# Expert pairs planned up to 12 slots behind the last scan, with GpSimdE storing the last ones, and earlier loads in the final stage

## The chip, the cores and the metric

The kernel runs on one core of one Trainium2 chip. The metric is device time in microseconds (us); lower is better. Everything is float32.

The engines are named here as in the profile: PE is TensorE (matmuls), PEld its weight loads, DVE is VectorE, ACT is ScalarE, POOL is GpSimdE, SP is SyncE, which here only issues transfers (DMAs). POOL also issues some. Each engine executes its instructions in program order.

## The reference, cut to what matters

Two batches of 256 channels by 64 x 64 positions (4096 tokens) go through a scan layer, then a layer of two scans (forward and flipped), then a mixture of 8 experts with soft weights:

```python
x = x + _L0_conv_ref(_gn(x), ...)            # selective scan, 256 inner channels
t = _to_tokens(x)
t = t + _L1_attn_ref(_ln_t(t), ...)          # two selective scans, 512 inner channels, one flipped
t = t + _L1_ffn_ref(_ln_t(t), ...)           # mixture of experts

def _L1_ffn_ref(x, ...):
    feat = jnp.mean(x, axis=0)               # mean over the two batches
    w = jax.nn.softmax(feat @ Wr + br, axis=-1)
    h = relu(bn(einsum('bfd,edh->bfeh', x, W1) + b1))
    h = relu(bn(einsum('bfeh,ehk->bfek', h, W2) + b2))
    y = jnp.einsum('bfeh,ehd->bfed', h, Wo) + bo
    return jnp.einsum('bfed,fe->bfd', y, w)  # weighted sum over the 8 experts
```

The point that shapes the kernel: an expert's three products depend on one batch's tokens alone, but the weight `w` of an expert for a token needs the mean over both batches, so it is known only when both batches have left the scans.

## The kernel before, in words

**Tiles.** Each batch's 4096 tokens are 8 chunks of 512 (`T`); a tile holds 128 partitions by 2 channel halves (`KC`) by 512. A *pair* is one expert applied to one chunk of one batch: 2 batches x 8 chunks x 8 experts = 128 pairs. Each pair has three products (layers 0, 1, 2 with W1, W2, Wo); each has two output halves `m`, and one half of one layer, an *entry* below, is four MATMUL instructions of the trace (two halves of the inner dimension, each float32 product showing as two MATMULs), so 24 per pair.

**First stage, the scans.** Six scan jobs (three per batch) are cut into chunks and *quads*; the main loop over `g` runs 640 quads with two *slots* each, 1280 slots in all. In each slot DVE does one scan instruction (L690), ACT the two exponentials it needs (L664), POOL or DVE the products before and behind it (L654, L699, L715), PE the sum over states (L723). All other work is put into slots by hand: `Slots.put(slot, queue, fn)` files a function under a slot and a queue, and in each slot the loop runs the queues `sp`, `pe`, the sums, `pe2`, the decays on ACT, `act`, the scan, `dve`, and `pool` in this order. The order is kept on each engine (`in_order`). A slot number is thus an order of issue and not a time: SP runs ahead of the others where no buffer holds it up.

**Features.** When a chunk of a flipped job is finished, `features` (L781 to L820) normalises it for the experts: a mean on PE, `fcen` on DVE, squares `fsq` on ACT (L799), a variance `fvar` on PE (L804), the root on ACT, the division on DVE, and a store to `nf_dram`. Offsets in slots are written out in one tuple. The very last flipped chunk (batch 1, chunk 0) has no such step.

**Experts beside the scans.** `experts` (L847) is a planner: it walks the slots up to `last` and keeps running balances of PE's and ACT's work (`PE_ROOM`, `PE_BEHIND`, `ACT_ROOM`, `ACT_BEHIND`) and of PSUM banks (`fits`). It places the six entries of each pair in order, and follows rules on distance: `waits` says that a layer's first entry comes at least 5 slots behind the same layer's last entry of the pair before (6 for layer 0 at a new chunk), because each layer's weights have one buffer (`ew0`, `ew1`, `ew2`), loaded 3 slots behind their last use. Complete pairs are kept (`put`) and given out by `emit_experts` (L905): weights by SP (L932), products on `pe2` (L912), relu or copy on ACT (L923, L921), and the unweighted result `eu`, one buffer, stored by SP into `u_dram` (L942) 3 slots behind the last entry. `early[b, c]` counts the pairs of a chunk that are done this way.

Behind the main loop come the last sum, the last gate and `sl.run_all(2 * nq, 2 * nq + 10)`, which runs what is filed in slots from 1280 on: before, the last chunk's output products (L759, L761 in slots 1283 and 1284), their copies (L776) and the store to `t_dram` (L777).

**Last stage, the rest of the experts.** The first stage's SBUF and PSUM pools close and new ones open. Chunks whose 16 pairs are all done form `whole`; the others form `rest`. For `rest` the remaining pairs run one after another on PE: `layer` (L1196) for layers 0 and 1 (L1201, relu L1205 on ACT), `weigh` (L1211) multiplies with the expert's weight on DVE (L1212), and `last_layer` (L1214) adds Wo's product into PSUM (L1220); a chunk's last pair adds PSUM to `x` (L1225) and stores. `waiting` holds the pairs between their layers and their last layer: a pair is weighed one pair later and goes through its last layer two pairs later.

Between the pairs the lists `side[i]` give out pieces of other work: `routes` (load features `n` by POOL L1086, sum over batches `nm` on POOL L1108, logits L1115, softmax, transposed weights, their store and broadcast load `wb` of 2 MB on POOL's queue L1144, L1146) for the chunks to come, and `sums` (load `x` L1156, bias L1163 to L1166, and for each pair done early `add_early` L1168: load `u` by SP L1170, times weight L1171 and added to `x` L1172 on DVE, then the store L1175). `u` has 3 buffers.

With the plan of before, 74 pairs are done beside the scans: `whole` is chunk 7, and chunk 6 has its batch 0 and two experts of batch 1. The last stage runs 54 pairs: 6 of chunk 6, then 8 (batch 1) of each of the chunks 5 to 0.

Of the kernel before, what the change touches and what calls it, by code (L numbers as in the profile page):

```python
# [42 lines left out]
F32 = mybir.dt.float32  # L43
# [4 lines left out]
P = 128  # L48
# [83 lines left out]
def hybrid_kernel(ctx: ExitStack, tc: tile.TileContext, a: dict, out: bass.AP):  # L132
# [53 lines left out]
    with ExitStack() as st:  # L186
# [594 lines left out]
        def features(b, c, v, s0):  # L781

            featured.add((b, c))

            def mean():
                v["ps"] = psp.tile([P, T], F32, tag="ps", name=f"fmean_{b}{c}")
                for k in range(KC):
                    nc.tensor.matmul(
                        v["ps"], mean_w, v["x"][:, k, :], start=(k == 0), stop=(k == KC - 1)
                    )  # L790

            def centre():
                v["cen"] = wk.tile([P, KC, T], F32, tag="cen", name=f"fcen_{b}{c}")
                nc.vector.tensor_tensor(v["cen"], v["x"], over_channels(v["ps"]), ALU.subtract)

            def square():
                for k in range(KC):
                    v["sq", k] = wk.tile([P, T], F32, tag="th", name=f"fsq_{b}{c}{k}", bufs=3)
                    nc.scalar.activation(v["sq", k], v["cen"][:, k, :], AF.Square)  # L799

            def variance():
                v["var"] = psp.tile([P, T], F32, tag="ps", name=f"fvar_{b}{c}")
                for k in range(KC):
                    nc.tensor.matmul(  # L804
                        v["var"], mean_w, v["sq", k], start=(k == 0), stop=(k == KC - 1)
                    )

            def divide():
                nc.vector.tensor_tensor(v["cen"], v["cen"], over_channels(v["var"]), ALU.mult)

            for d, queue, fn in (
                (0, "pe", mean), (1, "dve", centre), (2, "act", square), (3, "pe", variance),
                (4, "act", lambda: rsqrt(v["var"], v["var"], eps5)), (5, "dve", divide),
                (6, "sp", lambda: nc.sync.dma_start(nf_dram[b][:, c, :, :], v["cen"])),
            ):
                sl.put(s0 + d, queue, fn)
            sl.count(s0, 2, 0, (1,))
            sl.count(s0 + 1, 0, 2)
            sl.count(s0 + 3, 2, 2, (2,))
            ready.append((s0 + 8, b, c))  # L820

        def scales():

# [22 lines left out]

        def experts():  # L847

            last = 2 * nq - 6
            banks = sorted(sl.banks, key=lambda r: r[0])  # L850

            def fits(slot):
# [16 lines left out]
            def follows(l):  # L869

                k, m = divmod(len(times[l]), KC)
                if k == len(todo):
                    return None
                waits = [(l - 1, k * KC + 1, 2)] if l else []
                if m:
                    waits.append((l, k * KC, 0))
                elif k:

                    waits.append((l, k * KC - 1, 6 if l == 0 and todo[k][-1] == 0 else 5))
                    if l < 2:  # L880
# [24 lines left out]
        def emit_experts(put):  # L905
# [31 lines left out]
                n[b, c] = wk.tile([P, KC, T], F32, tag="en", name=f"en_{b}{c}")  # L937
                nc.sync.dma_start(n[b, c], nf_dram[b][:, c, :, :])

            def store(b, c, e, key):  # L940
                u = u_dram[b, c, e] = drp.tile([P, KC, T], F32, name=f"u_{b}{c}{e}")
                nc.sync.dma_start(u, key["u"])  # L942

            for b, c, e, times in put:
                key = {"tag": f"{b}{c}_{e}"}
# [5 lines left out]
                for l, (x, dst) in enumerate((("n", "h1"), ("h1", "h2"), ("h2", "u"))):  # L951
                    at = before.get(l, times[0] - 6) + 3
                    sl.put(at, "sp", lambda l=l, e=e, key=key: load_w(l, e, key["tag"]))
                    for m in range(KC):
# [1 line left out]
                        pe, act = layer(x, dst, l, m, e, key)  # L956
                        sl.put(slot, "pe2", pe)
                        sl.put(slot + 1, "act", act)
                sl.put(times[-1] + 3, "sp", lambda b=b, c=c, e=e, key=key: store(b, c, e, key))


        ready = []
# [92 lines left out]
            in_order()  # L1055
        emit_sum(g)
        emit_gate(i, steps[i][0].nj - 1)
        sl.run_all(2 * nq, 2 * nq + 10)
        assert not sl.at


    with ExitStack() as st:
# [12 lines left out]
        for i in range(NCH - 1, -1, -1):  # L1075
            (whole if all(first[b, i] == E for b in range(NB)) else rest).append(i)

        def load_n(i):

            for b in range(NB):  # L1080
                n[b, i] = mk.tile([P, KC, T], F32, tag="n", name=f"n_{i}{b}", bufs=6)
                if (b, i) in featured:
                    src = nf_dram[b][:, i, :, :]
                else:
                    src = t_dram[b][:, :, i * T : (i + 1) * T]
                nc.gpsimd.dma_start(n[b, i], src)  # L1086
# [107 lines left out]
            nc.sync.dma_start(we[name, e], a[name][e].rearrange("(k p) n -> p k n", p=P))  # L1194

        def layer(x, l, e, tag):  # L1196
            h = mk.tile([P, KC, T], F32, tag=f"h{l}", name=f"h{l}_{tag}", bufs=2 + l)
            for m in range(KC):
                ps = psp.tile([P, T], F32, tag="ps", name=f"hp{l}_{tag}_{m}")
                for k in range(KC):  # L1200
# [10 lines left out]
        def weigh(b, i, e, h):  # L1211
            nc.vector.tensor_tensor(h, h, over_channels(wb[i][:, e, :]), ALU.mult)  # L1212
# [39 lines left out]
        nc.sync.dma_start(bo, a["bo"])  # L1252
        layer_norm(rest[0])
        both(rest[0])
        weights = [("Wo", order[0])]
        for k in range(2, E):
            weights += [("W1", order[k]), ("W2", order[k]), ("Wo", order[k - 1])]
# [5 lines left out]
        for at, (b, i, e) in enumerate(pairs):  # L1263
# [6 lines left out]
                logits(i)  # L1270
            elif at == 1:
                spread(i)
            if waiting:
                weigh(*waiting[-1])
            waiting.append((b, i, e, h))
            if len(waiting) > 2:
                last_layer(*waiting.pop(0))
            done[i] += 1
            work = side[i] if at > 1 else []
# [111 lines left out]
```

## Time and profile before

| what | value |
|---|---|
| median of 3 runs | 5184.88 us (5181.89 to 5185.45) |
| the profiled execution | 5183.55 us |
| its span, first to last instruction | 5181.8 us |
| mean granted PE clock | 0.917 |
| first scan, last scan (start) | 61.1 us, 4498.2 us |
| mean time of one slot between them | 3.47 us |
| first matmul of the last stage | 4527.3 us |
| last matmul instructions end | 5176.4 us |

In section 2 of the page the span is cut into 40 slices of 130 us; in the first 34 of them DVE and POOL stand mostly at 9 tenths, and in the last 5 PE alone does. So the kernel has two stages with different limits, and a row of the whole page mixes them; it has to be read by window.

A row of the windows table gives for each engine its busy time and, in brackets, its number of instructions, then the granted PE clock, the busy share of the 16 DMA engines, and GB/s. A line of the chain gives the start, the length, and the piece of work that the end of the program hung on at that moment. A line of the waits gives the waiting engine and line, whom it waited for, the total in us, how often, and the longest.

### The profile page before, as it was taken

What the parts mean: (1) busy time and instruction counts of PE and PEld (TensorE: products, weight loads), DVE (VectorE), ACT (ScalarE), POOL (GpSimd) and SP (SyncE); (2) the same over time, 40 slices, a digit from 0 to 9 for tenths busy, and PEclk for the clock granted to TensorE, in tenths of its full rate; (3) what the DMA queues carried; (4) which work ended last, traced back from release to release, by engine and by line L of the source; (5) the groups of instructions that cost most, each with busy time, mean ns of one, the idle gap of its engine ahead of it and who ended that gap; (6) DMA issues with size and microseconds to landing.
All of it is one profiled execution on the core that took longest, in us unless ns stands there. A gap on an engine that the chain in (4) does not pass through costs nothing. (4 is left out here: it accounts for less than half of the span.)

```text
span 5181.8 us, 47299 instructions
## 1 busy us (share of the span) xinstructions
PE 4292.9 (83%) x14920; PEld 1483.9 (29%) x14920; DVE 4577.8 (88%) x3083; ACT 3681.3 (71%) x7462; POOL 4410.4 (85%) x1438
## 2 busy tenths in 40 slices
PE   5677677766668898888888888889899899689999
PEld 1222122222122233332222233223333333234444
DVE  6998999999999999999989999999999999746333
ACT  5778677777767888888887788888788888522332
POOL 5998999999999999999989999999999999611010
PEclk8888888887889999999999999999999999889999
DMA  4454433344334554555555544455544555354322
GB/s 176 154 178 163 154 127 139 129 152 154 135 131 160 195 185 164 182 171 196 191 185 177 191 159 174 155 181 191 178 165 165 173 183 175 117 189 155 111 104 77
DMA packets 314731, 834.47 MB, mean 161 GB/s; under 512 B 35240, under 2 KB 102064, under 8 KB 272496
## 3 DMA queue, kind: packets, MB, share of 16 engines
q1 hardware_dynamic: 310768, 806.15, 45.1%
q0 software_dynamic: 3712, 25.30, 1.3%
q8 instruction: 118, 1.93, 0.1%
q14 instruction: 133, 1.09, 0.1%
HBM read 647.18 MB, written 184.16 MB: 160 GB/s over the span
## 5 line engine op out<-in xcount | busy, mean ns | idle before, releaser
L654 POOL TENSOR_TENSOR bq<-rxdt,bc 128x2048 f32<-128x2048 f32 x640 | 2893.3, 4543 | 26.9 <-issue 11.8
L664 ACT ACTIVATE da<-rdt,w_a 128x512 f32<-128x512 f32 x2560 | 1756.5, 686 | 98.4 <-DVE bq L690 53.0
L690 DVE TENSOR_TENSOR_SCAN da<-da,h_state,bq 128x1024 f32<-128x1024 f32 x664 | 1559.2, 2348 | 63.8 <-ACT da L664 34.4
L715 POOL TENSOR_TENSOR bq<-bq,bc 128x2048 f32<-128x2048 f32 (+1 forms) x280 | 1180.0, 4214 | 22.5
L690 DVE TENSOR_TENSOR_SCAN bq<-da,h_state,bq 128x1024 f32<-128x1024 f32 x456 | 1058.6, 2338 | 20.3 <-ACT da L664 20.2
L723 PE MATMUL y<-bq,stack 128*32 128x512 f32 x5120 | 765.4, 691 | 347.4 <-POOL bq L715 324.1
L699 DVE TENSOR_TENSOR bq<-da,bc 128x1024 f32<-128x1024 f32 x760 | 926.5, 1219 | 15.9
L912 PE MATMUL e<-eh,ew 128*128 128x512 f32 x1184 | 578.6, 619 | 59.1 <-ACT eh L923 16.9
L709 ACT COPY h_state<-da 128x2 f32<-128x2 f32 x759 | 119.5, 157 | 680.0 <-DVE bq L699 678.5
L675 ACT ACTIVATE bq<-h_state,bq,a 128x1 f32<-128x1 f32 x1120 | 430.0, 384 | 0.7 <-POOL bq L654 0.2
L1205 ACT ACTIVATE h<-hp,of,sc 128x512 f32<-128x512 f32 x216 | 167.9, 778 | 347.4 <-PE hp L1201 330.3
L723 PEld LDWEIGHTS y<-bq,stack 128*32 128x32 f32 x5120 | 144.0, 118 | 906.1 <-POOL bq L715 461.1
L452 PE MATMUL conv<-xs,w_conv 64*64 64x512 f32 x2560 | 329.8, 604 | 24.4 <-ACT xs L436 21.4
L414 PE MATMUL z<-nx,w_in 128*128 128x512 f32 x640 | 324.7, 640 | 25.0 <-DVE sp L513 12.4
L414 PE MATMUL xs<-nx,w_in 128*128 128x512 f32 x640 | 317.5, 626 | 28.2 <-DVE xc L466 13.3
L912 PEld LDWEIGHTS e<-eh,ew 128*128 128x128 f32 x1184 | 214.2, 193 | 419.0 <-issue 209.0
L912 PE MATMUL e<-en,ew 128*128 128x512 f32 x592 | 286.1, 616 | 43.1 <-DVE sz L543 15.9
L761 PE MATMUL o<-sz,w_out 128*128 128x512 f32 x640 | 304.6, 616 | 0.0
L730 PE MATMUL y<-xc,w_d 128*128 128x512 f32 x320 | 193.6, 689 | 66.0 <-DVE sz L742 55.4
L517 POOL TENSOR_TENSOR xdt<-sp,xc 128x512 f32<-128x512 f32 x160 | 203.5, 1275 | 51.8 <-DVE sp L513 51.8
L923 ACT ACTIVATE eh<-e,of,sc 128x512 f32<-128x512 f32 x296 | 224.3, 770 | 30.5 <-PE e L912 29.9
L501 PE MATMUL dt<-dbc,w_dt 64*128 64x512 f32 x320 | 192.2, 695 | 41.2 <-ACT dbc L488 27.0
(138 smaller groups left out, 5045.5 us busy)
## 6 DMA issues: line engine op xcount, KB each, us to landing
rxdt<-xdtd SPq DMA_DIRECT2D x160, 1024.0 KB, 6.5
rdt<-dtd SPq DMA_DIRECT2D x160, 1024.0 KB, 6.3
bc<-bcd SPq DMA_DIRECT2D x384, 256.0 KB, 3.2
dtd<-sp SPq DMA_DIRECT2D x160, 256.0 KB, 3.6
xdtd<-xdt SPq DMA_DIRECT2D x160, 256.0 KB, 3.4
ew<-in_W SPq DMA_DIRECT2D x148, 256.0 KB, 4.9
u<-eu SPq DMA_DIRECT2D x74, 512.0 KB, 4.0
u<-u SPq DMA_DIRECT2D x74, 512.0 KB, 4.0
```

The costliest lines, as they stand in the source:

```text
L414: nc.tensor.matmul(ps, job.w["in", half][:, k, j * P : (j + 1) * P], rhs, start=(k == 0), stop=(k == KC - 1),)
L452: nc.tensor.matmul(v[r][64 * col : 64 * col + 64, :], job.w["conv"][rows, 2 * jp + j, k, :], ck["xs", jp][rows, j, k : k + T] if k < 4 els ...
L654: nc.gpsimd.tensor_tensor(bq[g], ck["rxdt", j], over_groups(ck["bc", 0, sg]), ALU.mult)
L664: nc.scalar.activation(da[g, h][:, k, :], cks[i]["rdt", j][:, q, :], AF.Exp, scale=steps[i][0].w["a"][:, j, q * SG + sg : q * SG + sg + 1],)
L675: nc.scalar.activation(bq[g][:, q, 0:1], job.h[:, j, sg, q : q + 1], AF.Identity, scale=cks[i]["a0", j][:, h, sg : sg + 1], bias=bq[g][:, ...
L690: nc.vector.tensor_tensor_scan(b if on_pool(g, h) else d, d, b, job.h[:, j, sg, 2 * h : 2 * h + 1] if c else 0.0, ALU.mult, ALU.add,)
L699: nc.vector.tensor_tensor(bq[g][:, two, :], d, cks[i]["bc", 1, sg].rearrange("p (o t) -> p o t", o=1).to_broadcast([P, 2, T]), ALU.mult,)
L715: nc.gpsimd.tensor_tensor(b, b, cks[i]["bc", 1, sg].rearrange("p (o t) -> p o t", o=1).to_broadcast([P, groups, T]), ALU.mult,)
L723: nc.tensor.matmul(y[i, j][q * CG : (q + 1) * CG, :], stack, bq[g][:, q, :], start=False, stop=(sg == SG - 1),)
L761: nc.tensor.matmul(v[m], job.w["out"][:, j, m * P : (m + 1) * P], ck["sz", j], start=False, stop=(j == job.nj - 1),)
L912: nc.tensor.matmul(ps, ew[l][:, k, m * P : (m + 1) * P], key[x][:, k, :], start=(k == 0), stop=(k == KC - 1),)
L923: nc.scalar.activation(key[dst][:, m, :], key["ps", l, m], AF.Relu, bias=of[:, l, e, m : m + 1], scale=sc[:, l, e, m : m + 1],)
```

## The change

1. In `features` the variance and all behind it move one slot later, and the chunk counts as ready at slot +9, not +8.
2. `experts` plans up to slot `2 * nq + 15`, not `2 * nq - 6`, so behind the last scan too, and lets a layer's first entry follow the same layer's last entry by 4 slots, not 5. `run_all` behind the loop runs up to `2 * nq + 24`.
3. A result `u` whose store falls behind slot `2 * nq - 8` is stored by GpSimdE's queue, not by SyncE's.
4. In the last stage `rest` is sorted by the number of pairs done; the features of the first whole chunk and of the second chunk of `rest` are loaded before the first pair; `h1` has 4 buffers, not 3; a pair waits three pairs, not two, for its last layer, and the first pairs are weighed later.

```diff
-                (0, "pe", mean), (1, "dve", centre), (2, "act", square), (3, "pe", variance),
-                (4, "act", lambda: rsqrt(v["var"], v["var"], eps5)), (5, "dve", divide),
-                (6, "sp", lambda: nc.sync.dma_start(nf_dram[b][:, c, :, :], v["cen"])),
+                (0, "pe", mean), (1, "dve", centre), (2, "act", square), (4, "pe", variance),
+                (5, "act", lambda: rsqrt(v["var"], v["var"], eps5)), (6, "dve", divide),
+                (7, "sp", lambda: nc.sync.dma_start(nf_dram[b][:, c, :, :], v["cen"])),
...
-            sl.count(s0 + 3, 2, 2, (2,))
-            ready.append((s0 + 8, b, c))
+            sl.count(s0 + 4, 2, 2, (2,))
+            ready.append((s0 + 9, b, c))
...
-            last = 2 * nq - 6
+            last = 2 * nq + 15
...
-                    waits.append((l, k * KC - 1, 6 if l == 0 and todo[k][-1] == 0 else 5))
+                    waits.append((l, k * KC - 1, 6 if l == 0 and todo[k][-1] == 0 else 4))
...
-                nc.sync.dma_start(u, key["u"])
+                by.dma_start(u, key["u"])
...
+                by = nc.gpsimd if times[-1] + 3 > 2 * nq - 8 else nc.sync
+                queue = "pool" if times[-1] + 3 > 2 * nq - 8 else "sp"
...
-        sl.run_all(2 * nq, 2 * nq + 10)
+        sl.run_all(2 * nq, 2 * nq + 24)
...
+        rest.sort(key=lambda i: sum(first[b, i] for b in range(NB)))
...
+            if (0, i) in n:
+                return
...
-            h = mk.tile([P, KC, T], F32, tag=f"h{l}", name=f"h{l}_{tag}", bufs=2 + l)
+            h = mk.tile([P, KC, T], F32, tag=f"h{l}", name=f"h{l}_{tag}", bufs=2 + 2 * l)
...
         both(rest[0])
+        for i in whole[:1] + rest[1:2]:
+            load_n(i)
...
-            if waiting:
-                weigh(*waiting[-1])
+            for p in {0: [], 1: [], 2: waiting[:1], 3: waiting[1:]}.get(at, waiting[-1:]):
+                weigh(*p)
             waiting.append((b, i, e, h))
-            if len(waiting) > 2:
+            if len(waiting) > 3:
                 last_layer(*waiting.pop(0))
```

More of the change, by code (lines that the diff above doesn't have):

```diff
@@ L938, in load_n, with store @@
                 nc.sync.dma_start(n[b, c], nf_dram[b][:, c, :, :])
-            def store(b, c, e, key):
+            def store(b, c, e, key, by):
                 u = u_dram[b, c, e] = drp.tile([P, KC, T], F32, name=f"u_{b}{c}{e}")
-                nc.sync.dma_start(u, key["u"])
+                by.dma_start(u, key["u"])
             for b, c, e, times in put:
@@ L958, in emit_experts @@
                         sl.put(slot + 1, "act", act)
-                sl.put(times[-1] + 3, "sp", lambda b=b, c=c, e=e, key=key: store(b, c, e, key))
+                by = nc.gpsimd if times[-1] + 3 > 2 * nq - 8 else nc.sync
+                queue = "pool" if times[-1] + 3 > 2 * nq - 8 else "sp"
+                sl.put(times[-1] + 3, queue, lambda b=b, c=c, e=e, key=key, by=by: store(b, c, e, key, by))
         ready = []
```

## The prediction

> **What bounds the kernel now.** I read the page first, for who is busy.
>
> ```profile
> PE 4292.9 (83%) x14920; PEld 1483.9 (29%) x14920; DVE 4577.8 (88%) x3083; ACT 3681.3 (71%) x7462; POOL 4410.4 (85%) x1438
> ...
> ew<-in_W SPq DMA_DIRECT2D x148, 256.0 KB, 4.9
> ```
>
> No engine stands out, because two stages are mixed. So next the windows of the last part:
>
> ```profile
> 4250.00:4502.00 252.00, 206.21 (x698) 70.93 (x700) 242.82 (x151) 192.88 (x398) 234.32 (x76) 0.92 0.44 153
> 4502.00:4527.00 25.00, 11.55 (x24) 4.20 (x24) 0.69 (x1) 1.17 (x2) 1.25 (x2) 0.70 0.36 121
> 4527.00:4700.00 173.00, 150.41 (x351) 65.80 (x352) 88.44 (x83) 43.91 (x61) 29.36 (x22) 0.89 0.57 201
> 4700.00:5182.00 482.00, 473.50 (x1146) 204.05 (x1145) 190.67 (x177) 144.48 (x193) 48.28 (x33) 1.00 0.30 104
> ```
>
> The columns are PE, PEld, DVE, ACT and POOL. Up to 4502 DVE is busy 96% and POOL 93%, PE 82%: the scans set the pace and PE has room. From 4527 PE alone is the bound (98% from 4700 on, DVE 40%). Between lie 25 us of crossing. A pair is nearly free in the first stage and costs its whole PE time in the last. The chain of waits shows the crossing:
>
> ```profile
> 4514.20 3.09 DMA t_dram<-xr
> ...
> 4520.01 7.27 DMA Wo<-in_Wo
> 4527.28 7.38 PE hp L1201 x10
> 4534.67 2.84 PE hp L1201 x6
> ...
> 4550.10 8.99 DMA wb<-w_dram
> 4559.11 1.24 DVE h L1212
> 4560.34 0.04 issue
> 4560.39 5.35 PE y L1220 x8
> ```
>
> All loads of the last stage wait for the last store out of the first stage's buffers; from that store's landing (4517.3) to the first matmul (4527.3) go 10.0 us. Later in the chain a pair looks like this:
>
> ```profile
> 4754.65 4.29 PE hp L1201 x10
> 4758.95 2.84 PE hp L1201 x6
> 4761.79 3.43 PE y L1220 x8
> ```
>
> That is 10.56 us per pair with PE gapless: my unit price. PE's own waits behind 4490, longest first:
>
> ```profile
> PE y L1220 <- DVE h L1212: 14.0, 3, 6.4
> PE hp L1201 <- DMA Wo<-in_Wo: 13.7, 1, 13.7
> PE lt L1115 <- POOL nm L1108: 6.6, 1, 6.6
> ```
>
> **How many pairs move.** I followed the planner's loop with the kernel's own counts. With the old constants it gives 74 pairs, as the trace has (1184 e<-eh matmuls at 16 per pair). With the new ones it gives 80: batch 0 whole, and chunks 7 and 6 of batch 1. Horizon alone would give 78, distance alone 79; moving the features a slot costs about one or two. Of the 36 more entries, 8 lie behind the last scan (slots 1280 twice, 1282, 1286 twice, 1287, 1290, 1291), about 9 more in the last ten slots before it, the rest spread. The last stage keeps 48 pairs, chunks 5 to 0.
>
> **The last stage, from its first matmul.** Before: 5181.8 - 4527.3 = 654.5. I account for it: 54 x 10.56 = 570.2; routing per chunk 1.69 (lt) + 0.44 (wt) + 1.91 (bi), x8 = 32.3; the norm of the last chunk 6.3 (1.93 + 1.98 + a wait of 2.4); half clock at the start 3.1 (7.38 against 4.29); from last matmul to end 5.3. Together 617.2, so 37.3 are stalls: the 14.0 and 6.6 above, wt on DVE 1.7, and matmuls at half clock behind these gaps, about 11.8 (5.35 and 5.40 where 3.43 is normal, 6.12 for 3.60, 7.21 for 4.29, 3.58 for 1.69, 1.03 for 0.44); 3.2 unassigned.
> - Six pairs less: -63.4 (48 x 10.56 = 506.9). Their 6 early adds stay off PE: DVE 2 x 1.22 each, 14.6 in all, beside PE.
> - Last layer one pair later: the first y waited for `wb` (landing at 4559.1, 31.8 behind the first matmul). With four pairs' layers, lt, wt and bi ahead of it, PE gets there after about 36. The four feature loads now issued early (2 MB, about 6 us at the 350 GB/s of that stretch) may delay `wb`; I keep 3 us of 8.3. The other two waits on weighed h (3.6 and 4.0, plus 2.0 of clock) come where a whole chunk's 16 adds crowd DVE: the weighing is some 8 us late in all, and a pair of slack is 10.6. But now there are two such chunks (7 and 6); I keep 4.
> - The features of the second and third chunk are loaded before the pairs: the 6.6 on nm, which was a 13.0 us load, goes, with its 4.8 of clock.
> - The wt stall with its clock I lower to 2.3. The sort of `rest` moves nothing (all six have 8 pairs done); a fourth h1 buffer costs only space.
>
> After: 506.9 + 32.3 + 6.3 + 3.1 + 5.3 + 3.2 + (3 + 4 + 2.3) = 566.4. Saved: 88.1.
>
> **The crossing.** Before, the last product by C ends at 4501.8 and the first new matmul starts at 4527.3. After, in PE's order: last sum to 4503.8, about 1 later for three entries queued just ahead of it; 8 entries x 1.72 (half of 3.43) = 13.7; the o products 2 x 4.31 = 8.6; about 1 for the relu between layers 1 and 2; 1 for ew2, which can load (4.9) only when the entry before has left its one buffer; 1.1 at half clock, as the o products lost before (9.7 for 8.6). That is 4530.2. Then the copy 0.6, the store's issue 0.54 (w_dram row on POOL) and landing. A POOL store of 512 KB does not exist before. Nearest row: POOL's loads of n, also 512 KB, 9.0 median, but beside 2 MB of weights; an SP store alone is 3.1. The Trainium skill (DMA: Bandwidth & Descriptors, "Anatomy of one DMA") fits POOL transfers as 2.0 us + bytes / 436 GB/s, which would be 3.2 here, and its Specifications speak against moving a store there: first byte about 1 us, against 0.6 from SP. By the row alone the crossing would be 6 longer; I take 4 (nothing else moves then), keeping 3.1 and 9. So landing at 4535.3, plus the same 10.0: first matmul 4545.3, **+18.0** (13 to 24). Behind the waiting POOL store stand only POOL's first loads of n, which wait for it anyway. On SP, the same store would have held up ew2; that is the only thing its move saves.
>
> On the clock, a rule against the hope that PE arrives warm: TensorE: Matmul & The Clock Gate, Part 1, says that one idle window of about 3.4 us puts PE back to half rate. The trace shows it behind every gap (7.38 for 4.29 after 13.7 idle). PE again idles about 14 us here, so the 3.1 of half clock stays; if it stayed warm the sum would be 3 less.
>
> **The scan stage.** 28 more entries inside it. Over stretches of 32 slots, time against entries in the trace gives about 0.05 us per entry, hidden under DVE and POOL: 1.4. In the last ten slots ACT gets nine or so more activations of 0.6 to 0.8 beside the last feature's table loads (2 x 1.28), in a stretch where ACT was busy 57%: bounded by 0 and 8, I take 4. The feature shift acts on this row:
>
> ```profile
> PE fvar L804 <- ACT fsq L799: 43.5, 15, 4.2
> ```
>
> PE stood 43.5 for squares it now needn't wait for; PE isn't the bound, so I give 3 of it (0 to 15). Its table loads, division and store only move by a slot, on queues with room. The shorter distance: 28 weight loads get 4 slots instead of 5 or more. SP issued loads at distance 5 about 9 us (median) before the using slot's scan; 3.5 less is 5.5, against 4.9 to land. Late ones stall PE, not DVE; 0 taken, up to 15. Sum: **+2** (-10 to +20).
>
> **Sum.** -88.1 + 18.0 + 2 = -68.1. The span becomes 5113.7 and the profiled execution 5183.55 - 68.1 = 5115.5; the median of the runs lies 1.3 above that execution, so **5117**. The forecast's own range is 5100 to 5132. A measurement of this kernel can tell about 0.2% (10 us) from no change.
>
> **Rivals.**
> - *Two crowded chunks keep PE waiting* (chance 0.13). Chunks 7 and 6 each bring 16 adds that DVE must do before it weighs. For it: the two 4 us waits of before, with DVE in between waiting on u loads (4.6 to 4.8 each) behind a store on SP. Against it: 10.6 more slack. If each chunk costs what it did (9.6, with clock) plus one u load more, it is about 14 x 2 instead of 4: 5141.
> - *The new stage's loads don't wait for the last u* (0.10), only for buffers they overlay. Then W and n arrive while PE still works, and the crossing grows by about 6, not 18: 5105. Against it: in the trace the first W on SP and the first n on POOL, different buffers, both waited for the same store.
> - *Weights come late* (0.04; slower). At distance 4 the single weight buffers leave 5.5 us by the median for a 4.9 us load. If each of the 28 came a slot late, and ACT's relu, queued ahead of the next exponentials, passed it whole to the scans, that is 28 x 3.5 = 98: 5215. It cancels the gain from 68 / 28 = 2.4 us per load on. Against it: PE has 18% room and no wait on an ew load stands among PE's longer waits now.
> - *The plan isn't what I worked out* (0.02): no more than 74 pairs; then only the stalls go, about 5160.
>
> The forecast has 0.71. The range 5098 to 5142 takes in the first two rivals and the bounds of the crossing and the scans. Three quarters of the late-weights case end slower, the rest within 0.2%; all other cases end faster. So faster by over 0.2%: 0.96; within: 0.01; slower: 0.03.
>
> **What would show it.** e<-eh matmuls x1280 and hp x768; last scan start within 4490 to 4518; first hp at about 4545, behind the landing of a u store from POOL's queue; no wait of lt on nm; y on h under 8 in sum; pairs at 10.56. Wrong if PE's waits in the scans show ew loads, if the last scan moves by over 20, if the store lands later than 9, or if the y waits come back in the chunks that bring 16 adds.

## The result, and the profile after

The changed kernel takes 5133.38 us (median of 4 runs, 5131.21 to 5136.12) against 5185.10 of the kernel before, run beside it (4 runs); the ratio is 0.9902 (95%: 0.9885 to 0.9919). It is faster, as forecast, and inside the range of 5098 to 5142, but by 51.7 us and not by 68: just above the forecast's own 5100 to 5132, and nearer to the first rival's 5141 than to 5117. The profiled execution took 5134.52 us, with a span of 5132.7, so all that follows is against 5181.8 of before.

The medians miss the forecast by 16 us, and the profiled spans by 19; three subtractions in the traces show where. The column "forecast" is the prediction's own step.

| stretch | before | after | change | forecast |
|---|---|---|---|---|
| start of the last scan | 4498.2 | 4502.4 | +4.2 | +2 |
| last scan to first matmul of the last stage | 29.1 | 41.3 | +12.2 | +18 |
| first matmul to the end | 654.5 | 589.0 | -65.5 | -88.1 |

The first two rows together came out 3.6 better than forecast; the last one 22.6 worse. The miss is in the last stage. (The first row is known to 2 or 3 us: in the seven profiles whose first stage is that of after, the last scan starts at 4499.5 to 4504.8.)

**The page of after.** 80 pairs left the scans' stage, as worked out: the page has e<-eh x1280 (16 a pair) and 192 relus h<-hp (four for each of 48 pairs). A row gives line, engine, operation and tiles, then busy us and mean ns, then the engine's idle time before it. The engines' busy shares hardly move (PE 83%, DVE 89%, POOL 86%).

```profile
L912 PE MATMUL e<-eh,ew 128*128 128x512 f32 x1280 | 626.1, 620 | 66.0 <-DVE sp L513 15.0
L1212 ACT ACTIVATE h<-hp,of,sc 128x512 f32<-128x512 f32 x192 | 149.1, 777 | 298.9 <-PE hp L1208 281.7
```

**The crossing.** The timelines of after (start, length, engine, line, operation, and in brackets the idle time before it and who ended it), PE's first and then POOL's:

```profile
4520.92 9.02 PE L912 MATMUL e<-eh,ew 128*128 128x512 f32 x20
4543.67 2.05 PE L1208 MATMUL hp<-n,W 128*128 128x512 f32 x2 [13.73 <-DMA W<-in_W]
```

```profile
4530.85 0.53 POOL L942 DMA_DIRECT2D u<-eu  x1 [6.61 <-ACT eu L921]
4534.70 1.06 POOL L1093 DMA_DIRECT2D n<-nf_dram  x2 [3.31 <-DMA u<-eu]
```

PE runs the last output products and, without a gap, 20 matmuls of experts to 4529.9; the copy follows, and POOL issues the last store at 4530.85. The chain of waits has its transfer, and what comes behind it (start, length, work):

```profile
4530.85 2.88 DMA u<-eu
...
4543.67 6.61 PE hp L1208 x10
```

The store lands 2.88 us after its issue begins, at 4533.73; 9.9 us later the first product starts (10.0 forecast), and its ten matmuls take 6.61 where 4.29 is normal. POOL's first n (L1093) waited for that store by its bracket, and so did SP's first weight load, by SP's own waits:

```profile
SPq L1201 <- DMA u<-eu: 10.5, 1, 10.5
```

So the rival "The new stage's loads don't wait for the last u" falls.

**The last stage, in windows of after** (PE, PEld, DVE, ACT, POOL busy with instructions, then the granted clock, DMA share, GB/s):

```profile
4600.00:4650.00 50.00, 49.96 (x129) 22.07 (x128) 18.32 (x19) 15.88 (x22) 8.66 (x7) 1.00 0.45 164
4650.00:4720.00 70.00, 55.94 (x134) 25.39 (x133) 53.63 (x48) 15.19 (x21) 9.82 (x7) 0.88 0.53 183
```

From 4600 to 4650 PE has no gap and the full clock. In the next 70 us it is idle for 14, the clock falls to 0.88, and DVE is busy 77%. Most of what DVE does not work there it waits for u (total, times, longest):

```profile
DVE u L1178 <- DMA u<-u: 13.8, 3, 7.0
```

SP issues these loads in order behind the output stores (L1182; in the chain one at 4669.8 and the load of u at 4670.2), and the stores wait for DVE's adds. DVE's lateness below is thus its adds together with these waits, and no run takes them apart. PE's own waits from 4490 on, in us in total, times, longest:

```profile
PE lt L1122 <- POOL nm L1115: 16.3, 2, 12.4
...
PE wt L1147 <- DVE w L1141: 3.3, 2, 1.7
...
PE hp L1208 <- ACT h L1212: 1.2, 1, 1.2
```

Left out are the one wait for the first loads (13.7) and one for the squares of the last chunk's norm (2.4), both of which before has too. The waits of y for weighed h (14.0 before) are gone, and the logits' wait for `nm`, which I expected to vanish, has grown from 6.6 to 16.3. Part of the chain shows what stands behind its longer half:

```profile
4694.30 1.24 DVE x L1179
4695.55 0.39 SPq L1182
...
4695.99 5.06 DMA x<-t_dram
...
4701.19 1.18 POOL x L1173
...
4705.82 3.29 POOL nm L1115
...
4709.15 3.59 PE lt L1122 x16
...
4715.40 5.91 PE hp L1208 x10
```

Read it downwards, with the code. DVE finishes the 16 early adds of chunk 7 at 4695.5. Only then can SP issue the store of its output (L1182), and behind that store, in SP's order, stands the load of x of chunk 4. POOL needs that x for its bias additions (L1173), and behind these, in POOL's order, stands the sum `nm` of the features of chunk 6, which is routed beside chunk 4's pairs: POOL ordered these features at 4646.9, and adds them only at 4705.8. PE's in-order stream comes to its logits before any of this is done. Behind the gap the logits take 3.59 for 1.69 and the next product 5.91 for 4.29, at half clock. So the chunk with 24 adds (16 of chunk 7 and 8 of its own) did keep PE waiting, but by the chain SP, POOL, logits, not by the weighing.

### The profile page after: what moved, and what is told of

It is laid out like the page before. It is cut to its first block, busy times and chain, and to the rows that moved or that the text cites. A ratio compares the mean times of both kernels' runs of the same rounds, so it can differ in the third digit from the quotient of the medians.

```text
span 5132.7 us, 47350 instructions
## 1 busy us (share of the span) xinstructions
PE 4283.0 (83%) x14920; PEld 1485.7 (29%) x14920; DVE 4581.7 (89%) x3088; ACT 3681.3 (72%) x7474; POOL 4410.3 (86%) x1442
## 4 chain that ended last, share of the span: by engine, by line
DVE 20%; PE 15%; ACT 10%; issue 4%; POOL 3%; DMA 2%; SPq 0%; DVEq 0%; POOLq 0%; ACTq 0%
DVE da L690 9%; PE hp L1208 5%; DVE bq L699 5%; ACT da L664 4%; PE y L1227 2%; PE e L912 2%; DVE bq L690 2%; POOL bq L654 2%; PE conv L452 1%; POOL bq L715 1%; PE y L723 1%; ACT bq L675 1%; DVE x L1179 1%; DVE u L1178 1%; ACT eh L923 1%
## 5 line engine op out<-in xcount | busy, mean ns | idle before, releaser
L723 PE MATMUL y<-bq,stack 128*32 128x512 f32 x5120 | 759.4, 687 | 317.4 <-POOL bq L715 297.3
L912 PE MATMUL e<-eh,ew 128*128 128x512 f32 x1280 | 626.1, 620 | 66.0 <-DVE sp L513 15.0
L723 PEld LDWEIGHTS y<-bq,stack 128*32 128x32 f32 x5120 | 143.6, 119 | 876.7 <-POOL bq L715 404.9
L1212 ACT ACTIVATE h<-hp,of,sc 128x512 f32<-128x512 f32 x192 | 149.1, 777 | 298.9 <-PE hp L1208 281.7
L912 PEld LDWEIGHTS e<-eh,ew 128*128 128x128 f32 x1280 | 230.3, 193 | 452.0 <-issue 219.4
L452 PE MATMUL conv<-xs,w_conv 64*64 64x512 f32 x2560 | 332.6, 613 | 21.9 <-ACT xs L436 18.9
L414 PE MATMUL z<-nx,w_in 128*128 128x512 f32 x640 | 323.8, 639 | 18.7 <-DVE sp L513 10.6
L912 PE MATMUL e<-en,ew 128*128 128x512 f32 x640 | 308.3, 613 | 23.9 <-DVE fcen L809 7.8
L923 ACT ACTIVATE eh<-e,of,sc 128x512 f32<-128x512 f32 x320 | 242.1, 768 | 36.7 <-PE e L912 36.2
L690 DVE TENSOR_TENSOR_SCAN da<-da,bq 128x1024 f32<-128x1024 f32 x96 | 219.4, 2286 | 6.5 <-ACT da L664 3.6
```

Of the source, the lines that this page charges most:

```text
L414: nc.tensor.matmul(ps, job.w["in", half][:, k, j * P : (j + 1) * P], rhs, start=(k == 0), stop=(k == KC - 1),)
L452: nc.tensor.matmul(v[r][64 * col : 64 * col + 64, :], job.w["conv"][rows, 2 * jp + j, k, :], ck["xs", jp][rows, j, k : k + T] if k < 4 els ...
L690: nc.vector.tensor_tensor_scan(b if on_pool(g, h) else d, d, b, job.h[:, j, sg, 2 * h : 2 * h + 1] if c else 0.0, ALU.mult, ALU.add,)
L723: nc.tensor.matmul(y[i, j][q * CG : (q + 1) * CG, :], stack, bq[g][:, q, :], start=False, stop=(sg == SG - 1),)
L912: nc.tensor.matmul(ps, ew[l][:, k, m * P : (m + 1) * P], key[x][:, k, :], start=(k == 0), stop=(k == KC - 1),)
L923: nc.scalar.activation(key[dst][:, m, :], key["ps", l, m], AF.Relu, bias=of[:, l, e, m : m + 1], scale=sc[:, l, e, m : m + 1],)
```

## Experiments

My first theory was this chain: the adds make SP's queue late, SP makes POOL late, POOL makes PE late. The rivals were that DVE's lateness itself is enough, by whichever consumer meets it first, and that the pair of depth in `waiting` was not worth what I gave it.

**e1: x loaded ahead of chunk 7's adds.** The load of the chunk's own x goes ahead of the whole chunk's adds; its bias additions stay behind them in the list of side work:

```diff
                 for j in whole[at - 1 : at]:
-                    work += sums(j)
+                    other = sums(j)
+                    work += [other[0], now.pop(0)] + other[1:]
```

> The changed kernel, with one thing moved: in the two chunks that bring a whole chunk's 16 early adds, the load of the chunk's own x is issued right behind the load of the whole chunk's x, not behind the whole chunk's last store. Queue theory (PE's 16.3 us at the logits come from GpSimdE's sum nm standing behind its bias add, which waits for an x load that SyncE issues only behind a store that waits for all 16 adds): the wait of lt on nm falls from 16.3 to under 3, the half-rate matmuls behind it (about 8 us) go too, the span falls by 18 to 24, to about 5111, and the median to about 5112. Crowding theory (VectorE's 16 adds are themselves the limit): the wait only changes its name, the last-layer product then waits for the weighed h by about as much, and the time falls by less than 6.

Measured: 5141.76 us, ratio to before 0.9916 (0.9901 to 0.993), 8.4 above after and not 18 to 24 below it; neither theory had forecast a loss. PE's waits from 4495 on:

```profile
PE wt L1147 <- DVE w L1141: 18.0, 2, 16.4
...
PE hp L1208 <- ACT h L1212: 9.0, 1, 9.0
```

The wait for `nm` is gone, so that chain was real; but the time came back one step later. The softmax of the logits is on DVE, behind the same adds; PE now waits for its weights `w` (16.4), and ACT, which stands in the softmax's exponential, keeps relus waiting (9.0). One wait of 4.0 at y for the weighed h is back as well. The theory "the queues are late" falls as the whole cause: DVE is late, and each of its consumers with less slack than the weighing meets it. POOL's bias additions now also run beside DVE's adds of chunk 7, and both get longer (last section), which may be part of why this is slower than after.

**e2: two pairs of depth, not three.**

```diff
-            h = mk.tile([P, KC, T], F32, tag=f"h{l}", name=f"h{l}_{tag}", bufs=2 + 2 * l)
+            h = mk.tile([P, KC, T], F32, tag=f"h{l}", name=f"h{l}_{tag}", bufs=2 + l)
...
-            for p in {0: [], 1: [], 2: waiting[:1], 3: waiting[1:]}.get(at, waiting[-1:]):
+            for p in waiting[-1:]:
...
-            if len(waiting) > 3:
+            if len(waiting) > 2:
```

> The changed kernel with the old depth: a pair is weighed one pair later, goes through its last layer two pairs later, h1 with 3 buffers. Queue theory: the third pair of depth is what took the waits on the weighed h away (14.0 us before, none after); without it the first product waits for wb again (6 to 9) and each crowded chunk makes it wait once or twice for 3 to 4, but these waits then lie partly on the same time as the 16.3 at the logits; the time rises by 8 to 18, to about 5146. Crowding theory: the crowded chunks lose the same time whatever the depth, only the wait for wb comes back: plus 6 to 9, about 5141.

Measured: 5145.87 us, 0.9924 (0.9907 to 0.9941), 12.5 above after. PE's waits:

```profile
PE y L1227 <- DVE h L1219: 25.7, 5, 8.4
...
PE lt L1122 <- POOL nm L1115: 2.1, 1, 2.1
```

One of the five waits at y is another matter: the first y of the stage waits 8.4 for `wb`, as in before, with 2.1 of half clock behind it. The other four, 17.3, lie in the two crowded chunks, and PE, having waited there, waits only 2.1 at the logits and not 16.3: it is one lateness, collected by the first consumer in PE's order. So the third pair is worth about 12, but some 10.5 of it is the first y; in the crowded chunks it saves 2 by the medians and about 5 by the two profiled runs.

**e3: every u stored by SyncE.** `by = nc.sync` and `queue = "sp"` for all stores.

```diff
-                by = nc.gpsimd if times[-1] + 3 > 2 * nq - 8 else nc.sync
-                queue = "pool" if times[-1] + 3 > 2 * nq - 8 else "sp"
+                by = nc.sync
+                queue = "sp"
```

> The changed kernel with all stores of u on SyncE's queue. The prediction said that the move to GpSimdE saves only this: on SyncE a store waiting for eu holds up the weight loads behind it, ew2 above all. Two stores stand ahead of such loads near the end, so the crossing grows by 0 to 6 us, the time to 5133 to 5139. If GpSimdE's stores cost more themselves (a slower start of their transfer), the time falls by 1 to 3 instead.

Measured: 5132.9 us, 0.9899 (0.9885 to 0.9914), the same as after within 0.5. The mechanism is there, in the chain of waits of e3, but with 1.1 us of PE's waiting as its price:

```profile
4522.55 0.34 SPq L942
...
4522.98 3.33 DMA ew<-in_Wo
...
4530.77 2.67 DMA u<-eu
```

The weights of the last entries go out behind the store, as forecast, and yet the last u leaves at 4530.77, as in after (4530.85). The choice of the queue is worth nothing that can be measured.

**e4: no pairs behind the last scans.** The horizon of before, and no sort of `rest`; all else of the change; 77 pairs.

```diff
-            last = 2 * nq + 15
+            last = 2 * nq - 6
...
-        rest.sort(key=lambda i: sum(first[b, i] for b in range(NB)))
```

> The changed kernel planned only up to six slots before the last scan, as before, so 77 pairs and none behind the scans (chunk 6 then keeps three pairs and comes first, the sort is left out). The three pairs cost 3 x 10.6 = 31.7 in the last stage. The crossing from the last scan to the first matmul of the last stage shrinks by the 12 that it grew. One crowded chunk less: if the queue theory holds, one of the two waits at the logits goes too (4 to 12, with clock up to 16), though the short first chunk with 23 pieces of side work in three pairs may bring others (up to 10). Sum: plus 4 to plus 20, time about 5145.

Measured: 5165.6 us, 0.9963 (0.9948 to 0.9978), 32.2 above after, well over the 4 to 20 expected. Its first matmul of the last stage comes at 4529.4, 14.3 earlier than in after, and its three pairs more cost 31.7; that makes 17.4, and the other 14.8 are stalls. What I had not counted enough is that chunk 6 is then one short chunk of three pairs into which its own sums and the routing of two chunks must be pressed; all of these waits but the 7.1 of one at the logits stand there:

```profile
PE lt L1121 <- POOL nm L1114: 21.7, 3, 8.7
...
PE wt L1146 <- DVE w L1140: 8.0, 2, 6.2
```

So nearly half of what the pairs behind the last scan bring in this plan comes from closing the chunk, not from the pairs' own PE time (taken at 10.56 each).

**e5: the adds of a whole chunk spread over two.** DVE's lateness as the cause predicts that the gaps go when no chunk gets 24 adds. Of each whole chunk's sums, batch 0 goes beside one chunk of `rest` and batch 1 beside the next; the routing of the second whole chunk (6) follows one chunk later, and `wb` has a third buffer. Nothing is taken out, but three things change at once.

```diff
-            wb[i] = mk.tile([P, E, T], F32, tag="wb", name=f"wb_{i}")
+            wb[i] = mk.tile([P, E, T], F32, tag="wb", name=f"wb_{i}", bufs=3)
...
-            if at:
-                for j in whole[at - 1 : at]:
-                    work += sums(j)
+            if at and (at - 1) // 2 < len(whole):
+                other, cut = sums(whole[(at - 1) // 2]), E + 3
+                work += other[:cut] if at % 2 else other[cut:]
...
-            for j in whole[at : at + 1] + after:
+            for j in (whole[at // 2 : at // 2 + 1] if at % 2 == 0 else []) + after:
```

> The changed kernel, with the 32 early adds of the two whole chunks spread: one batch's 8 adds of chunk 7 each into chunks 4 and 3, of chunk 6 into chunks 2 and 1, with a third buffer for wb. No chunk has more than 16 adds, about 51 us of VectorE work in its 88. Crowding theory (VectorE falls 16 to 20 us behind where a chunk has 24 adds, and PE meets that at the next thing that needs VectorE or what waits for it: nm through the bias add, the softmax w, ACT behind the softmax): all these waits go, 16.3 on nm and the 10 to 14 of waits and half clock around them; the span falls by 20 to 26, to about 5109, and the median to about 5110. Queue theory in its first form (the x load's place): most of the same, but a wait of lt on nm stays wherever a bias add stands ahead of it, 3 to 6 in each of four chunks, and the gain is under 12.

Measured: 5113.46 us, 0.9861 (0.9847 to 0.9876), 19.9 below after. The stretch of the gaps, and the only wait of PE in the last stage besides the first loads' and the norm's:

```profile
4650.00:4720.00 70.00, 69.94 (x175) 30.50 (x174) 46.77 (x42) 21.01 (x29) 10.09 (x7) 1.00 0.48 169
```

```profile
PE lt L1122 <- POOL nm L1115: 8.7, 1, 8.7
```

PE is gapless at full clock where it had stood 14 us. First matmul to the end is 570.1, within 4 of the 566.4 forecast for after: with most of DVE's lateness away the prediction's sum for this stage, which keeps 9.3 for stalls, holds. The wait of 8.7 that is left stands beside chunk 3's pairs, where two chunks are routed now (6 and 2). In after it is chunk 4 that routes two chunks (6 and 3) beside 24 adds, and it has the longer of the two waits. So the adds are not the whole of it: how much of the 20 us comes from spreading them and how much from moving the routing, this run does not tell.

**e6: e5, and what the first matmul needs is loaded first.** W1 of the first expert and `n` of batch 1 are issued first, on SP.

```diff
-        load_n(rest[0])
-        for name, e in [("W1", order[0]), ("W2", order[0]), ("W1", order[1]), ("W2", order[1])]:
-            load_w(name, e)
+        for b in range(NB):
+            n[b, rest[0]] = mk.tile([P, KC, T], F32, tag="n", name=f"n_{rest[0]}{b}", bufs=6)
+        load_w("W1", order[0])
+        nc.sync.dma_start(n[1, rest[0]], nf_dram[1][:, rest[0], :, :])
+        load_w("W2", order[0])
+        nc.sync.dma_start(n[0, rest[0]], nf_dram[0][:, rest[0], :, :])
+        for name in ("W1", "W2"):
+            load_w(name, order[1])
```

> e5_adds_spread, and at the start of the last stage W1 of the first pair and the features of its batch go out first, on SyncE, the other batch's features and the next weights behind them. From the last u's landing to the first matmul it took 9.5 us, while 2 MB came in together; the first matmul needs 0.75 MB of them. If the bytes set that time, the first matmul comes 3 to 5 earlier and the time is 3 to 5 below e5_adds_spread; if the later weights then come late, PE waits in the first or second pair and it is 0 to 2.

Measured: 5111.54 us, 0.9857 (0.9842 to 0.9872). The crossing is 36.3 us against e5's 40.8, but the whole gains only 2. In the profiled runs the last scan starts 1.1 later, which the edit does not touch, and the last stage takes 1.8 more, 1.5 of it a wait at y. It has the lowest median here, with e5 inside its interval.

**e7: the last stage's part of the change alone**, in the kernel before (74 pairs, distance 5, horizon and features as before): the loads ahead, the fourth `h1`, three pairs of depth.

```diff
-            h = mk.tile([P, KC, T], F32, tag=f"h{l}", name=f"h{l}_{tag}", bufs=2 + l)
+            h = mk.tile([P, KC, T], F32, tag=f"h{l}", name=f"h{l}_{tag}", bufs=2 + 2 * l)
...
+        for i in whole[:1] + rest[1:2]:
+            load_n(i)
...
-            if waiting:
-                weigh(*waiting[-1])
+            for p in {0: [], 1: [], 2: waiting[:1], 3: waiting[1:]}.get(at, waiting[-1:]):
+                weigh(*p)
...
-            if len(waiting) > 2:
+            if len(waiting) > 3:
```

> The kernel before with the last stage's changes alone (loads ahead, three pairs of depth, h1 with 4 buffers): 74 pairs, chunk 6 first. The wait for wb (6.4 and 1.9 of clock) and those on nm and w in chunk 6 (8.3 and 7.9 of clock) go. The one crowded chunk (5, with chunk 7's adds) lost 9.6 at the weighed h before; by the crowding theory it then loses about 16 to 20 at the logits, as the first crowded chunk of the changed kernel. Sum: 10 to 18 less, about 5171. By the prediction's reckoning, where a third pair of depth covers the crowding, 24 less: 5161.

Measured: 5165.28 us, 0.9962 (0.9947 to 0.9977): 20 of the 52 us. No wait of y for weighed h is left; lt waits 1.4 for `nm`, wt 2.4, hp 4.5 for relus. The forecast for all stalls together was 88.1 - 63.4 = 24.7; the other 32 come with the planner's part. But the 20 do not come from the crowded chunk, which is chunk 5 here. They come from the first y, which no longer waits for `wb` (6.4, and 1.9 of clock), and from chunk 6. In chunk 5 the 9.6 that before lost at the weighed h are lost again at the logits (1.4) and, with a late softmax on ACT, at the relus behind them (3.7), with half clock (5.38 for 3.60, 6.42 for 3.87), 9.5 in all:

```profile
4678.41 5.38 PE L1203 MATMUL hp<-n,W 128*128 128x512 f32 x8
4687.48 6.42 PE L1203 MATMUL hp<-h,W 128*128 128x512 f32 x8 [3.70 <-ACT h L1207]
```

**e8: no features loaded ahead**, all else of the change.

```diff
-        for i in whole[:1] + rest[1:2]:
-            load_n(i)
```

> The changed kernel without the features of two chunks loaded ahead. The logits of chunk 7 then wait for nm as before (6.6 and 4.8 of clock); wb comes some us earlier, which no one waits for. Sum: 5 to 11 more, about 5141. If the loads ahead delay something on the path, it is 0 to 3 less.

Measured: 5133.33 us, 0.9901 (0.9884 to 0.9917), no different from after; 5 to 11 more was expected. PE waits 17.7 at the logits, in two places of which the longest has 11.5, the place seen in after:

```profile
PE lt L1122 <- POOL nm L1115: 17.7, 2, 11.5
```

The 6.6 wait of before came in a short first chunk of six pairs. With eight pairs in the first chunk the load seems to have the time it needs anyway. The two next runs fit that: neither loads features ahead, and PE waits nothing at the logits with seven pairs in the first chunk (e9), and 27.8 with three (e10). No run changes this length alone.

**e9: the features' shift alone**, in the kernel before; it leaves room for 73 pairs.

```diff
-                (0, "pe", mean), (1, "dve", centre), (2, "act", square), (3, "pe", variance),
-                (4, "act", lambda: rsqrt(v["var"], v["var"], eps5)), (5, "dve", divide),
-                (6, "sp", lambda: nc.sync.dma_start(nf_dram[b][:, c, :, :], v["cen"])),
+                (0, "pe", mean), (1, "dve", centre), (2, "act", square), (4, "pe", variance),
+                (5, "act", lambda: rsqrt(v["var"], v["var"], eps5)), (6, "dve", divide),
+                (7, "sp", lambda: nc.sync.dma_start(nf_dram[b][:, c, :, :], v["cen"])),
```

> The kernel before with the feature steps alone moved by a slot: 73 pairs. Read from the start of the last scan (4498.2 before). In the changed kernel the scans of slots 448 to 736, with the first batch's features, took 6 us less; if the shift does that, it is 6 to 10 less here. The one pair less costs 10.6 in the last stage. Time 5180 to 5190. If the shift does nothing, the last scan stays within 2 and the time is about 5195.

Measured: 5170.97 us (9 runs), 0.9972 (0.9962 to 0.9982). The last scan starts at 4489.9, 8.3 earlier, and the total falls by 14, with a pair more in the last stage; 5180 to 5190 was expected. The scans' part came as expected. The rest is the last stage: the profiled run takes 652.6 from its first matmul where before took 654.5, so that stalls fell by more than the pair costs (no wait at the logits, 8.9 and not 14.0 at y). Most of that lies in the first chunk, which has seven pairs here: luck of the plan, as I read it, and not the shift's work. For the scans, the rows that moved are ones I did not read, of DVE's waits and not of PE's. Before, up to 4498:

```profile
DVE da L690 <- issue: 19.6, 31, 1.5
...
DVE fcen L809 <- ACT fvar L180: 5.5, 3, 2.0
...
DVE sp L513 <- ACT h_state L709: 3.9, 6, 1.0
```

With the shift alone the first of them is 9.3 in 17, and the second is absent: the division that completes a feature had waited on DVE, the bound of that stage, for ACT's root. The third grew to 10.2 in 11. Together that is 9.5 less, near the 8.3; but the largest part is "issue", for which the profile names no releaser, so the cause of it is not shown.

**e10: the distance of 4 alone**, in the kernel before, with the horizon cut so that 77 pairs fit and none runs late.

```diff
-            last = 2 * nq - 6
+            last = 2 * nq - 18
...
-                    waits.append((l, k * KC - 1, 6 if l == 0 and todo[k][-1] == 0 else 5))
+                    waits.append((l, k * KC - 1, 6 if l == 0 and todo[k][-1] == 0 else 4))
```

> The kernel before with the distance of 4 slots alone, planned up to slot 1262, so that 77 pairs lie inside the scans and none behind (chunk 6 keeps three). Read from the start of the last scan. In the changed kernel the scans from slot 1024 on took 8 us more; if the shorter distance and the denser pairs do that (late weights, or ACT), the last scan comes 5 to 15 later than before, and waits of PE on ew loads or of VectorE on ACT grow. If not, it stays within 2. The time itself is not compared: the short first chunk of three pairs brings waits of its own in the last stage.

Measured: 5190.88 us (12 runs), 1.0013 (1.0005 to 1.0022): three pairs more beside the scans, and no gain. The last stage takes 655.0 from its first matmul, with three pairs less, against 654.5 before: what the pairs save there is lost again in stalls (waits of 27.8 at the logits, all in the short first chunk of three pairs, and 19.9 at y). So this total says nothing of the distance. The last scan starts 9.4 later, at 4507.6, and the lateness has reached 4 by slot 736 and 12 by slot 1184, so it is not made at the end. Weights are not late:

```profile
PE e L912 <- DMA ew<-in_W: 0.5, 2, 0.3
```

What it costs the scans in detail I did not find: DVE's waits for the exponentials are no longer in sum than before (63.5 against 63.6).

**e11: e6, with a chunk's own x load and bias ahead of the other chunk's adds.**

```diff
+            if at and len(after):
+                work += now[:2]
+                now = now[2:]
```

> e6_spread_first_loads, and in chunks 4 to 1 the chunk's own x load and bias come first among the side work, ahead of a whole chunk's adds and of all routing. In e5 and e6 one wait is left: in chunk 3 the bias adds, nm and the logits were given out between the same two pairs, and PE waited 8.7 for nm behind two bias adds, with some 4 of half clock behind it. Crowding and order together: with the bias adds done long before, that wait goes and the time falls by 9 to 13, to about 5101. If the wait comes from VectorE's lateness and not from what was given out together, it stays.

Measured: 5114.04 us, 0.9868 (0.9851 to 0.9884), no gain over e6, where 9 to 13 was expected. The wait for `nm` (8.7) is gone, and 5.7 at wt and 1.8 at a relu stand in its place: e1 again, on a smaller scale.

## Why the prediction was right, and where it was not

**Right: the mechanism of the move and the count.** 80 pairs by the planner's loop; the six moved pairs worth 10.56 each where PE is the bound; the normal pair of after has the same 4.29, 2.84 and 3.43. e5 puts the stage within 4 us of its sum.

**The crossing: right in kind, 6 too long.** The prediction had PE done at 4530.2 and it was done at 4529.9, with the scans 4.2 later than before; so the tail is shorter than I built it. The last sum ended 4.7 behind the start of the last scan (at 4507.1, the end of L723 in PE's timeline), where I had 6.6, with 1 for entries queued ahead of it. From there to the end of the experts' products it is 22.8 where I added up 25.4: the pauses of about 1 each for a relu and for the weights, and the slow clock of the o products, did not come, since PE had no gap. The store took 2.88 from the start of its issue where I had 4.5 (0.54 and 4). These three make 6.2; the step from PE's end to the store's issue took 0.3 more than I had, which leaves the 5.8. For the store the row of the nearest kind, 9.0 beside 2 MB of weights, was the wrong neighbour; the 3.1 of SP's lone store was the right one, and so was the fit named in the prediction (3.2).

**The scans: right in sum by luck, through two terms that cancel.** I gave 3 us of gain to the shift and nothing to the distance. Alone they measured about -8 and +9 (the second with three pairs more in it). The shift was judged by PE's wait for the variance, which did not get shorter: in after its largest part alone, fvar behind DVE's sp (L513), is 55.1 up to 4503. What moved was DVE's waits (e9).

**The step that failed** is "Last layer one pair later", in its words "the weighing is some 8 us late in all, and a pair of slack is 10.6. But now there are two such chunks (7 and 6); I keep 4." The lateness was there, and the slack held where I looked: y has no waits. But the same late DVE also feeds the store in front of SP's loads, and the softmax in front of the weights, and these had under a pair of slack. With what else I kept for stalls I had 9.3; the trace has 16.3 at the logits, 3.3 at wt, 1.2 at a relu, and some 10.4 of half clock behind them (3.58 for 1.69 twice, 1.02 for 0.44, eight matmuls of hp at 5.26, 5.29 and 6.25 for 3.60), together 31.2. The difference of 21.9 is nearly all of the miss of 22.6.

By chunk the sum is plainer. A crowded chunk lost 9.6 before (at y) and 9.5 in e7 (at the logits and relus). In after, chunk 3 loses 9.6 (3.9, 1.2 and 4.5 of clock) and chunk 4 loses 21.5 (12.4, 3.3 and 5.8 of clock). So the added depth hid little of a crowded chunk: nothing in e7 against before, and 2 to 5 for two chunks in e2. The price for two was at least twice 9.6, and not 4. Chunk 4, which also routes two chunks, lost 12 more. The rival "Two crowded chunks keep PE waiting" had the right place and, at 24 us above the forecast's price, nearly the right size; only its form, that PE waits at y, was wrong. The two chunks that bring a whole chunk's 16 adds (4 and 3) hold the two waits at the logits, 12.4 and 3.9. The features' row (6.6 with 4.8 of clock) was also mis-assigned: by e8 the loads ahead are not what took it away. And half clock does not stand behind every gap, as the prediction says it does. In before, behind a gap of 3.58, the product ran at its normal pace (3.60):

```profile
4664.49 3.70 PE L1220 MATMUL y<-h,Wo 128*128 128x512 f32 x8 [3.58 <-DVE h L1212]
```

**What stays open.** Why the distance of 4 costs the scans 9 us. The shares of e1's 8.4 us between DVE's longer adds and ACT's wait were not separated. Nor were the parts of DVE's adds, of its waits for u behind SP's stores and of the second routing in the 21.5 us of chunk 4: no run moved the stores or the routing alone.

## What to carry to other kernels

When work on an in-order engine is going to be late, list every consumer of that engine, through the queues behind it too, and set the lateness against the slack of each: more depth for the main consumer only hands the wait to the next. Side work of a fixed size is better spread over the stretches that must hide it than reordered within one: reordering (e1, e11) moved the wait, spreading (e5, with one chunk's routing moved too) removed most of it, 20 us of a total of 72. And look for the value of a small shift in the waits of the engine that bounds that stage, not of the one whose wait looks longest.

## What the runs showed of the hardware that I had not expected

Transfers of 512 KB issued by POOL and by SP, alone, are alike: 2.88 (after) and 2.67 us (e3) from the start of the chain's piece, beside 3.09 for SP's store of `t_dram` in before. So a lone store is priced by a lone store and not by the engine that issues it.

DVE's operations and POOL's, on SBUF alone, lengthen each other when they run together. In e1, DVE's timeline while POOL adds the bias (start, length, line):

```profile
4685.90 1.22 DVE L1219 TENSOR_TENSOR h<-h,wb 128x1024 f32<-128x1024 f32 x1
...
4688.29 3.25 DVE L1179 TENSOR_TENSOR x<-x,u 128x1024 f32<-128x1024 f32 x1
4691.46 3.36 DVE L1178 TENSOR_TENSOR u<-u,wb 128x1024 f32<-128x1024 f32 x1
```

```profile
4688.05 5.69 POOL L1173 TENSOR_TENSOR x<-x,bi 128x1024 f32<-128x1024 f32 x2 [38.72 <-ACT bi L1171]
```

Three additions and products in a row (4688.3 to 4698.1) took 3.25 to 3.36 where 1.22 is normal, and POOL's two took 5.69 for 4.63. The three cost DVE about 6.2 more, while POOL's three pieces of work (the two, and 3.33 for `nm`, 2.33 alone) lasted 9. The Trainium skill (SBUF — State Buffer, "Who interferes with whom") says that a DVE instruction with two SBUF inputs contends with a GpSimd one that reads SBUF, and these rows agree. In the kernel of after POOL's additions waited for x until chunk 7's adds were done, but they met the adds of chunk 4 itself:

```profile
4703.63 3.27 DVE L1178 TENSOR_TENSOR u<-u,wb 128x1024 f32<-128x1024 f32 x1 [6.97 <-DMA u<-u]
```

By contrast, DVE's n<-n,mean_m, which reads one input from PSUM, kept its 1.22 at 4958.39 in after, beside POOL's additions from 4957.15 on.
